# Reserving a PSUM bank only where it is used, and moving the feed-forward's statistics behind the softmax division

## The chip, the cores and the metric

The kernel runs on one core of a Trainium2 chip. The metric is the device time of one execution in microseconds, taken as the median of several runs; less is better. The engines named below are TensorE (PE in the profile), VectorE (DVE), ScalarE (ACT), GpSimd (POOL) and the queue of SyncE (SP), which issues the DMAs of the main path.

## The reference, cut to what matters

The input has two batches of 256 times, 128 bands and 128 channels, in float32. Three residual blocks follow one another: causal attention over time, attention over bands with a mask that lets each band see 16 neighbours on either side, and a feed-forward with 512 hidden channels.

```python
B, T, FB, C = (2, 256, 128, 128)
H_T, H_F, BAND = (4, 4, 16)
INNER = 4 * C
xt = _ln(x, ln_t_w, ln_t_b).transpose(0, 2, 1, 3)
x = x + _mha(xt, t_wi, t_bi, t_wo, t_bo, H_T, cm).transpose(0, 2, 1, 3)
xf = _ln(x, ln_f_w, ln_f_b)
x = x + _mha(xf, f_wi, f_bi, f_wo, f_bo, H_F, bm)
xn = _ln(x, ln_n_w, ln_n_b)
h = jax.nn.gelu(xn @ w1.T + b1, approximate=False)
x = x + (h @ w2.T + b2)
```

## The kernel before

**Groups.** The work is cut into groups of 4 tiles of 128 x 128. First come 128 groups of time attention (`OverTime`). Then come 16 runs, each of 8 groups of band attention (`OverBands`) followed by the 8 groups of the feed-forward (`FeedForward`) on the same data; the feed-forward group that stands 8 places behind a band group reads that group's result `x2`. The change touches only the 16 runs.

**Steps.** `run` (line 1058) is one loop over steps n. Each step calls parts of several groups, and every instruction is pinned to the order in which it is emitted on its engine (`InOrder`, line 872). In this document the steps of one run are numbered 0 to 15: band groups are at home in steps 0 to 7, feed-forward groups in steps 8 to 15. Step 8 is the turn (`turn` in the code, line 1083).

**What one band step does.** TensorE: scores of group n (into four banks `sp`), the softmax sums `rp` and weighted values `op` of group n-1 (`weigh`, line 803; the profile's `bank<-pf,ones` and `bank<-pf,v`), the output product `yp` of group n-2 (`bank<-wn,oT`), then queries `qp`, keys `kp` and values `vp` of group n+1. ScalarE: four exponentials, then logarithm and exponential of `rp` (`invert`, line 607), then copies of queries, keys and values. POOL: the two small instructions of `root` (line 456) for feed-forward group n+4, and then six selects that mask the exponentials of heads 0 to 2 (`first_mask`, line 789). `root` comes first in POOL's order. Head 3 is masked by VectorE instead.

**VectorE in a band step**, in order: `first_function` (line 779, `bank<-bank,band`, the mask of head 3), `normalize` (four `xh`) and `turn` (one transpose `z`) for group n+3, `statistics` (line 447: four `stats`, four `mv`) of feed-forward group n+5, `finish` (line 641, `x<-bank,x`) of group n-2, and `divide` (line 620) of group n-1. `divide` has three instructions: `bank<-bank,r` works inside the bank of `rp`; `u<-bank,r` is the last that reads this bank; `oT<-bank,u` reads the bank of `op` and makes the input of the next step's output product. In steps 0 to 2 group n+5 is still a band group, so there are no feed-forward statistics; in steps 3 to 8 there are. In step 8 an exact reciprocal of `rp` (3.32 us, `invert_exactly`) comes before `finish` and `divide`.

**What follows the statistics.** The `mv` of group g, made at step g-5, are read by POOL's `root` at step g-4; VectorE normalizes the group at step g-3.

**Banks.** PSUM has 8 banks. On these steps they are handed out in turn (`turn_of_bank`, line 915), and a bank is written again only when all earlier users are through. `weigh` of a band group takes two turns ahead, before `rp` and `op`: one for `yp`, which this step's `output` uses, and one for `qp`, which this step's `queries_keys` uses (lines 579, 637 and 806). In steps 7 and 8 no band group follows whose queries could use the second. The bank reserved in step 8 stays in `path.held` and is taken in step 15 by the queries of the next run's first group.

The turns of steps 7 and 8 are then, in order: step 7, four `sp`, `yp`, `qp` (unused), `rp`, `op`; step 8, four `hp` (hidden layer of feed-forward group 8), `yp`, `qp` (unused there), `rp`, `op`. A step with 8 turns gives each tile the bank that its counterpart had a step earlier.

Of the kernel before, what the change touches and what calls it, by code (L numbers as in the profile page):

```python
# [427 lines left out]
class Group:  # L428
# [121 lines left out]
    def weigh(self):  # L550
        pass
# [95 lines left out]
def rows_of(h):  # L647
    return slice(h * D, (h + 1) * D)
# [95 lines left out]
def time_scores(old, new):  # L744


    if new is not None:
        new.first_tiles()
    if old is not None:
        old.second_tiles()  # L750
    for kind, h, s, e in TIME_ORDER:
        if kind == "s" and old is not None:
            old.second_scores(int(h), int(s), int(e) * HALF)
        if kind == "f" and new is not None:
            new.first_scores(int(h), int(s), int(e) * HALF)


class OverBands(Attention):


    which = 1
    by_vector = 1

    def scores(self, heads):
# [38 lines left out]
    def weigh(self):  # L803
        path = self.path

        path.held = dict(yp=path.turn_of_bank(), qp=path.turn_of_bank())
        self.rp = path.bank([P, NT * P], "rp")
        for h in range(H):
            path.tensor.matmul(
                self.rp[rows_of(h), :], path.k.ones[:, 0:D], self.p[:, h].rearrange("p i q -> p (i q)"),  # L810
                start=True, stop=True,
            )
        self.op = path.bank([P, NT * P], "op")
        for i in range(NT):
            c = slice(i * P, (i + 1) * P)
            for h in range(H):
                r = rows_of(h)
                path.tensor.matmul(self.op[r, c], self.v[:, i, r], self.p[:, h, i, :], start=True, stop=True)
# [68 lines left out]
class BoundedPath:  # L887
# [170 lines left out]
    def run(self, x, out):  # L1058
        groups = list(self.groups(x, out))

        def do(n, *names):
            if 0 <= n < len(groups):
                for name in names:
                    getattr(groups[n], name)()

        def at(n, kind):
            return 0 <= n < len(groups) and isinstance(groups[n], kind)

        def do_at(n, kind, *names):
            if at(n, kind):  # L1070
                do(n, *names)


        run0 = [i for i in range(len(groups)) if at(i, OverBands)][: RUN // NT]
        due = dict(zip(run0, (-5, -4, -4, -3, -1, 0, 1, 2)))
        due = {n: [i for i in run0 if run0[0] + due[i] == n] for n in range(-12, len(groups) + 2)}
        A = RUN // NT

        self.scalar.preload_act_table_set(EXP_SET)
        for n in range(-12, len(groups) + 2):  # L1080
            feeds = [at(n - 2 + i, FeedForward) for i in range(5)]
            bands = [at(n - 2 + i, OverBands) for i in range(5)]
            turn = feeds[2] and bands[1]
            old, new = (groups[i] if at(i, OverTime) else None for i in (n, n + 1))
            if bands[2] and feeds[1]:
                self.scalar.preload_act_table_set(EXP_SET)
            do_at(n + 4, FeedForward, "root")
            do(n, "first_half", "first_function", "first_mask")
            if n >= 0:
                do_at(n + 5, OverTime, "statistics")  # L1090
            if old is not None or new is not None:
                time_scores(old, new)
                b = self.banks
                Attention.place = dict(rp=b["b0"], op=b["b3"], yp=b["a1"], qp=b["a2"], kp=b["b1"], vp=b["b2"])
            else:
                Attention.place = {}
            if old is not None:
                old.second_weights(old.late)
            if new is not None:
                new.first_weights(new.early[:1])  # L1100
            if old is not None:
                old.second_weights(old.early)
                old.mask_second()
                old.add(0)
                old.add(1)
            if new is not None:
                new.first_weights(new.early[1:])
            if n >= 0:
                do_at(n + 5, OverTime, "root_in_bank")
            if turn:  # L1110
                do(n, "second_half", "second_function")
            do_at(n + 3, OverTime, "fetch")
            do_at(n + 2, (OverBands, FeedForward), "fetch")

            for i in (2 * n + 12, 2 * n + 13) if n < -2 else (n + 10,) if n < 2 else ():
                if i >= NT:
                    do(i, "load")
            if n < -8 or n >= 0:
                do(n + 12, "load")
            if n >= 0:  # L1120
                for i in due[n]:
                    do(i, "statistics")
            do_at(n + 3, (OverBands, FeedForward), "normalize", "turn")
            do_at(n + 4, OverTime, "normalize", "turn")
            if n >= 0:
                do_at(n + 5, OverTime, "refine")
            if n < 0:
                do(n + 5, "statistics")
            do_at(n + 5, FeedForward, "statistics")
            if n == -4:  # L1130
                self.fold_rest()
                self.warm()
            do(n - 1, "weigh")
            do(n - 1, "invert_exactly" if turn else "invert")
            if new is not None:
                new.first_weights(new.late)
            if bands[2] or turn or old is not None:
                do(n - 2, "output", "finish")
            do(n - 1, "divide")
            if not turn:  # L1140
                do(n, "second_half", "second_function")
            if n in run0:
                do(n, "bias")
            if not bands[2] and old is None:
                do_at(n, FeedForward, "bias")
                do_at(n + A, OverBands, "bias")
                if at(n - 1, FeedForward) and at(n - 2, OverBands):
                    do_at(n + A - 1, OverBands, "statistics", "root")
                if not turn:
                    do_at(n + A, OverBands, "statistics", "root")  # L1150
            do_at(n + 2, OverTime, "queries_keys", "take_query", "take_key")
            do_at(n + 1, OverBands, "queries_keys", "take_query", "take_key")
            if n < 0:
                do_at(n + 5, OverTime, "root_by_scalar", "refine")
            for i in due[n]:
                do(i, "root_by_scalar", "refine")
            do_at(n, OverTime, "bias")
            if new is not None:
                new.mask_first()
            if not bands[2] and not turn and old is None:  # L1160
                do(n - 2, "output", "finish")
            do_at(n + 2, OverTime, "values", "take_values")
            do_at(n + 1, OverBands, "values", "take_values")
            if old is not None or new is not None:

                b = self.banks
                self.banks = dict(
                    a1=b["a1"], a2=b["a2"], b0=b["a0"], b3=b["a3"], a0=b["b0"], a3=b["b1"], b1=b["b3"], b2=b["b2"]
                )
# [69 lines left out]
```

## Time and profile before

| | before |
|---|---|
| median of 3 runs | 2682.34 us (2681.44 to 2683.59) |
| the profiled execution | 2680.03 us, of which the span of its trace is 2678.2 us |
| granted TensorE clock | 0.999 |
| VectorE busy | 2190.0 us (82%) |
| POOL busy | 1951.5 us (73%) |
| ScalarE busy | 1856.2 us (69%) |
| one run of 16 steps, start to start (1282.67 to 1390.10 us) | 107.43 us |

Busy times are shares of the whole span, in which three kinds of work follow one another, so they don't say which engine limits a stage. The starts of one recurring instruction say it better: the interval between two `bank<-pf,ones` is what a band step costs TensorE, and the interval between two `bank<-bank,band` is what it costs VectorE.

### The profile page before, as it was taken

What the parts mean: (1) busy time and instruction counts of PE and PEld (TensorE: products, weight loads), DVE (VectorE), ACT (ScalarE), POOL (GpSimd) and SP (SyncE); (2) the same over time, 40 slices, a digit from 0 to 9 for tenths busy, and PEclk for the clock granted to TensorE, in tenths of its full rate; (3) what the DMA queues carried; (4) which work ended last, traced back from release to release, by engine and by line L of the source; (5) the groups of instructions that cost most, each with busy time, mean ns of one, the idle gap of its engine ahead of it and who ended that gap; (6) DMA issues with size and microseconds to landing.
All of it is one profiled execution on the core that took longest, in us unless ns stands there. A gap on an engine that the chain in (4) does not pass through costs nothing.

```text
span 2678.2 us, 156630 instructions
## 1 busy us (share of the span) xinstructions
PE 2639.5 (99%) x68662; PEld 1801.7 (67%) x68662; DVE 2190.0 (82%) x6708; ACT 1856.2 (69%) x3620; POOL 1951.5 (73%) x2297
## 2 busy tenths in 40 slices
PE   7999999999999999999999999999999999999998
PEld 5666666666666666666666666666666667666665
DVE  6888898988889996967868769688687696886874
ACT  6999999999999874664755746647557466475573
POOL 4999999999999886766667657666676576666762
PEclk9999999999999999999999999999999999999999
DMA  6556555555555544445445444454454544544533
GB/s 151 151 150 157 145 154 155 149 150 152 150 151 150 132 115 125 121 115 132 111 120 132 112 123 121 119 132 110 121 133 109 123 124 114 136 109 122 131 96 83
DMA packets 471511, 347.09 MB, mean 130 GB/s; under 512 B 43296, under 2 KB 405152, under 8 KB 470816
## 3 DMA queue, kind: packets, MB, share of 16 engines
q1 hardware_dynamic: 469568, 335.92, 48.9%
q8 instruction: 540, 8.85, 1.5%
q14 instruction: 155, 1.27, 0.2%
q10 hardware_dynamic: 1248, 1.05, 0.2%
HBM read 169.03 MB, written 167.77 MB: 126 GB/s over the span
## 4 chain that ended last, share of the span: by engine, by line
PE 80%; DVE 15%; DMA 2%; issue 1%; SPq 1%; ACT 0%; DVEq 0%; ACTq 0%
PE bank L882 80%; DVE xh L882 3%; DVE bank L882 3%; DVE stats L882 2%; DVE z L882 2%; DVE u L882 2%; DMA xnT<-turned 1%; DVE x L882 1%; DMA turned<-z 1%; DVE mv L882 1%; SPq L882 1%; DVE oT L882 0%; ACT p L882 0%; DVE vy L882 0%; DVE res L882 0%
## 5 line engine op out<-in xcount | busy, mean ns | idle before, releaser
L882 ACT ACTIVATE hT<-bank,b 128x512 f32<-128x512 f32 x512 | 347.0, 688 | 536.1 <-PE bank L882 518.0
L882 POOL TENSOR_SCALAR_AFFINE_SELECT pf<-pf 128x512 f32<-128x512 f32 x768 | 478.0, 637 | 244.8 <-ACT pf L882 218.4
L882 DVE TENSOR_SCALAR xh<-x,mv,rstd 128x160 f32<-128x160 f32 x1536 | 596.6, 430 | 14.2
L882 PEld LDWEIGHTS bank<-w2T_sb,hT 128*32 128x32 f32 x16384 | 459.3, 110 | 62.9 <-issue 38.8
L882 PE MATMUL bank<-xnT,wf 128*32 128x512 f32 x4096 | 487.6, 592 | 3.0 <-ACT p L882 3.0
L882 PE MATMUL bank<-w2T_sb,hT 128*32 128x128 f32 x16384 | 477.2, 273 | 0.4 <-ACT hT L882 0.2
L882 PE MATMUL bank<-xnT,w1f 128*32 128x512 f32 x4096 | 474.5, 592 | 0.0
L882 ACT ACTIVATE p<-bank 128x512 f32<-128x512 f32 (+1 forms) x1024 | 430.6, 494 | 37.9 <-PE bank L882 26.7
L882 POOL TENSOR_SCALAR_AFFINE_SELECT p<-p 128x1024 f32<-128x1024 f32 (+2 forms) x384 | 364.5, 950 | 83.5 <-ACT p L882 75.0
L882 DVE TENSOR_TENSOR res<-bank,res 128x512 f32<-128x512 f32 x256 | 175.8, 687 | 289.7 <-PE bank L882 230.2
L882 PEld LDWEIGHTS bank<-wf,xnT 128*32 128x32 f32 x8192 | 234.0, 110 | 155.8 <-issue 103.0
L882 POOL TENSOR_TENSOR p<-p,p 128x512 f32<-128x512 f32 x256 | 324.3, 1289 | 10.7
L882 PE MATMUL bank<-qT,kT 32*64 32x80 f32 (+4 forms) x16384 | 323.7, 273 | 4.0 <-DVE oT L882 2.4
L882 DVE BATCH_NORM_STATS2 stats<-x 128x6 f32<-128x128 f32 x1536 | 326.3, 274 | 0.1
L882 PEld LDWEIGHTS bank<-qT,kT 32*64 32x64 f32 x16384 | 275.9, 131 | 58.2 <-ACT kT L882 48.4
L882 ACT ACTIVATE pf<-bank 128x512 f32<-128x512 f32 x512 | 267.0, 602 | 50.7 <-PE bank L882 49.0
L882 DVE STREAM_TRANSPOSE z<-xh 128x512 f32<-128x512 f32 x384 | 273.2, 711 | 13.5
L882 PEld LDWEIGHTS bank<-xnT,w1f 128*32 128x32 f32 x4096 | 156.8, 110 | 189.3 <-issue 158.3
L882 POOL TENSOR_SCALAR rstd<-mv 128x4 f32<-128x4 f32 x248 | 56.7, 229 | 311.0 <-DVE mv L882 309.8
L882 PE MATMUL bank<-wn,oT 128*32 128x128 f32 x8192 | 272.0, 273 | 0.0
L882 POOL TENSOR_TENSOR rstd<-rstd,mhalf 128x4 f32<-128x4 f32 x248 | 256.9, 1036 | 20.7
L882 PE MATMUL bank<-wf,xnT 128*32 128x128 f32 x8192 | 271.6, 273 | 0.0
(97 smaller groups left out, 3653.3 us busy)
## 6 DMA issues: line engine op xcount, KB each, us to landing
turned<-z SPq DMA_DIRECT2D x1536, 64.0 KB, 2.5
xnT<-turned SPq DMA_DIRECT2D x384, 256.0 KB, 3.2
x<-in_x SPq DMA_DIRECT2D x128, 256.0 KB, 4.3
x<-res SPq DMA_DIRECT2D x256, 128.0 KB, 2.4
x<-x SPq DMA_DIRECT2D x128, 256.0 KB, 4.3
out<-res SPq DMA_DIRECT2D x256, 128.0 KB, 2.5
w1T_sb<-in_w1T ACTq DMA_DIRECT2D x1, 256.0 KB, 5.7
w2T_sb<-in_w2T ACTq DMA_DIRECT2D x1, 256.0 KB, 7.3
```

What stands on the lines that cost most here:

```text
L882: return self.tc.keep_in_program_order(emit(*args, **kwargs))
```

## The change

There are two edits. In `weigh`, a band group takes a turn for `yp` always, and one for `qp` only where the group two places on is also a band group: in steps 1 to 6 of a run, not in steps 7 and 8. The queries of a run's first group take the bank in turn, since none is held for them.

In steps 3 to 8, `statistics` of the feed-forward is emitted behind `divide` of group n-1, where before it stood ahead of `weigh`. On VectorE the order of a band step becomes `first_function`, `xh`, `z`, `x`, the three instructions of `divide`, `stats`, `mv`. In the feed-forward steps from 9 on it stays where it was. No instruction is added or left out.

```diff
@@ class OverBands
     which = 1
+    follow = ("yp",)
     by_vector = 1
@@ def weigh(self):
-        path.held = dict(yp=path.turn_of_bank(), qp=path.turn_of_bank())
+        path.held = {name: path.turn_of_bank() for name in self.follow}
         self.rp = path.bank([P, NT * P], "rp")
@@ def run(self, x, out):
+        for i in range(len(groups) - 2):
+            if at(i, OverBands) and at(i + 2, OverBands):
+                groups[i].follow = ("yp", "qp")
@@ in the loop over n
-            do_at(n + 5, FeedForward, "statistics")
+            if not bands[2] and not turn:
+                do_at(n + 5, FeedForward, "statistics")
...
             if bands[2] or turn or old is not None:
                 do(n - 2, "output", "finish")
             do(n - 1, "divide")
+            if bands[2] or turn:
+                do_at(n + 5, FeedForward, "statistics")
```

## Prediction

> **What bounds the kernel now.** I read the page first: its busy times, then TensorE's groups.
>
> ```profile
> PE 2639.5 (99%) x68662; PEld 1801.7 (67%) x68662; DVE 2190.0 (82%) x6708; ACT 1856.2 (69%) x3620; POOL 1951.5 (73%) x2297
> ...
> L882 PE MATMUL bank<-pf,ones 128*32 128x512 f32 x1024 | 136.7, 604 | 12.4 <-DVE u L882 12.4
> ```
>
> TensorE is idle for 38.7 us of the 2678.2. By the page's slices 13 to 20 us of that lie in the first fortieth of the span and some in the last, so a change to the runs has little to gain. One idle time recurs: 12.4 us ahead of the softmax sums `rp`, released by VectorE's `u`. The view of waits gives its count.
>
> ```profile
> PE bank L882 <- DVE u L882: 12.8, 17, 0.8
> ```
>
> One of the 17 (0.35 us at 934 us) lies in the time attention; the other 16 are one per run. The timeline of one run, TensorE first (start, duration, instructions), shows where, and the reader should look at the starts:
>
> ```profile
> 1426.14 1.20 PE L882 MATMUL bank<-qT,kT 32*64 32x80 f32 x64
> 1427.27 1.06 PE L882 MATMUL bank<-pf,ones 128*32 128x512 f32 x8
> 1428.15 1.06 PE L882 MATMUL bank<-pf,v 128*32 128x128 f32 x32
> 1429.03 1.06 PE L882 MATMUL bank<-wn,oT 128*32 128x128 f32 x32
> 1429.90 3.62 PE L882 MATMUL bank<-xnT,w1f 128*32 128x512 f32 x32
> 1434.31 1.06 PE L882 MATMUL bank<-pf,ones 128*32 128x512 f32 x8 [0.79 <-DVE u L882]
> ```
>
> The idle 0.79 us is at step 8, the turn. The same view of VectorE, from step 7's first instruction on:
>
> ```profile
> 1428.28 0.69 DVE L882 SCALAR_TENSOR_TENSOR bank<-bank,band 128x512 f32<-128x512 f32 x1
> 1428.88 1.60 DVE L882 TENSOR_SCALAR xh<-x,mv,rstd 128x160 f32<-128x160 f32 x4
> 1430.51 0.71 DVE L882 STREAM_TRANSPOSE z<-xh 128x512 f32<-128x512 f32 x1
> 1431.15 0.83 DVE L882 BATCH_NORM_STATS2 stats<-x 128x6 f32<-128x128 f32 x4
> 1431.90 0.36 DVE L882 BATCH_NORM_AGGREGATE mv<-stats 128x2 f32<-128x6 f32 x4
> 1432.18 0.66 DVE L882 TENSOR_TENSOR x<-bank,x 128x512 f32<-128x512 f32 x1
> 1432.75 0.69 DVE L882 TENSOR_TENSOR bank<-bank,r 128x512 f32<-128x512 f32 x1
> 1433.47 0.69 DVE L882 SCALAR_TENSOR_TENSOR u<-bank,r 128x512 f32<-128x512 f32 x1
> 1434.20 0.69 DVE L882 TENSOR_TENSOR oT<-bank,u 128x512 f32<-128x512 f32 x1
> ```
>
> VectorE has no gap. From `bank<-bank,band` to the next it takes 6.53 us in steps 3 to 7 of every run, while TensorE's steps take 6.3 (6.32 from step 4's `bank<-pf,ones` to step 5's and from there to step 6's, as means over the runs): VectorE is the slower engine there, falls 0.2 us further behind per step, and is caught at step 8. The last view is POOL in steps 6 and 7:
>
> ```profile
> 1425.82 0.23 POOL L882 TENSOR_SCALAR rstd<-mv 128x4 f32<-128x4 f32 x1 [0.26 <-DVE mv L882]
> 1426.13 1.04 POOL L882 TENSOR_TENSOR rstd<-rstd,mhalf 128x4 f32<-128x4 f32 x1
> 1428.10 3.94 POOL L882 TENSOR_SCALAR_AFFINE_SELECT pf<-pf 128x512 f32<-128x512 f32 x6 [0.92 <-ACT pf L882]
> 1432.35 0.23 POOL L882 TENSOR_SCALAR rstd<-mv 128x4 f32<-128x4 f32 x1 [0.31 <-DVE mv L882]
> 1432.66 1.03 POOL L882 TENSOR_TENSOR rstd<-rstd,mhalf 128x4 f32<-128x4 f32 x1
> 1433.66 1.28 POOL L882 TENSOR_TENSOR res<-x,rows_sb 128x512 f32<-128x512 f32 x1
> ```
>
> The root is done before the exponentials arrive, so the selects wait for ScalarE, and end at 1432.04, over 2 us before TensorE reads them at 1434.31.
>
> **What the Trainium skill says.** "PSUM — Partial Sum Buffer", section "Engine vs sequencer instructions": the queues of ScalarE, VectorE and GpSimd are strict first-in first-out, and matmuls start in program order. The trace agrees: POOL's selects never pass the root ahead of them, and a late `rp` holds all of step 8's products. "Perfetto Trace Analysis", section "Optimization Strategy", takes a gap that repeats on the saturated engine as a hint at too few buffers; the 16 gaps of 0.61 to 0.84 us on a bank fit. "SBUF — State Buffer", section "SBUF: two separate sides": VectorE and GpSimd share a port pair as an exclusive lock, which a VectorE instruction with two SBUF inputs takes. In this trace, at 919.73 us, a 128x4 `vy` beside a POOL select took 1.01 us against 0.16 elsewhere. Feed-forward statistics have one SBUF input and took 0.83 us for four beside selects (1424.62) and 0.86 beside an idle POOL (1464.75); this is why I let durations stand when the order changes.
>
> **The change part by part.** *The bank.* Before, steps 7 and 8 take 8 turns each, so step 8's `rp` falls on step 7's `rp`, whose last reader is `u`: 1433.47 + 0.69 + 0.15 of release = 1434.31. After, they take 7 each. Eight turns back from step 8's `rp` is now step 7's `yp`, free with `x` at 1432.84; `op` gets step 7's `rp`, but is written 0.85 later; `yp` gets the fourth `sp`. TensorE could start `rp` at 1429.90 + 2 x 1.72 (what 16 products of that kind take, 1436.91 to 1438.63) = 1433.34. With this edit alone `op`'s wait sets 1434.31 - 0.85 = 1433.46, a gain of 0.85. Of this step 9 takes some back: its output product, at 1443.84 before, would come to 1442.99, and `oT` of step 8 ends at 1442.60 + 0.43, with release 1443.18. So 0.66 us per run, 10.6 in all. The bank in step 15: the queries get one last used in step 14, and the four `sp` of step 0 get banks whose readers ran in step 15, ahead of the keys which the scores need anyway; I cost it at nothing.
>
> *The statistics.* VectorE's sum stays; 1.03 us (1432.18 - 1431.15) move from ahead of `x` to behind `oT`. So `x`, `u` and `oT` end 1.03 earlier, and `bank<-bank,band` stays where it was. `u` is then free for step 8 at 1433.28, and the second `oT` at 1442.0, so neither of the two waits above is left, whichever bank is used. It also frees 0.17: step 7's scores at 1426.14 take 1.20 instead of some 1.0, since their third bank is step 6's `yp`, read by `x` until 1426.31. Does a moved instruction now wait? `x` would start at 1431.15 and its product ended at 1430.09; `bank<-bank,r` at 1431.72 and ScalarE's `r` ended at 1430.75. In step 3, where VectorE is least behind, 1405.04 against 1404.72 and 1405.62 against 1405.24. No. Neither moved nor passed instructions issue a DMA here (a band group has no store), so SP's queue is untouched.
>
> What it delays is POOL: `root` stands ahead of the selects, and now waits for `mv` made at the end of VectorE's step. Call the start of step p's `bank<-bank,band` zero. The `mv` end at 0.08 (as `mv` now end 0.08 after `x` starts), plus 0.09 release (1432.26 to 1432.35), plus 1.31 from `rstd` to POOL's next start, plus 3.94 for six selects, plus 0.15 release to TensorE, taken from `u`: 5.57. Heads 0 and 1 of the sums can issue before, which I put at 0.02. So TensorE's next `rp` comes at 5.55 at the earliest. In step 7's frame before it came at 1434.31 - 1428.28 = 6.03 (6.02 to 6.04 in all 16 runs). Unhindered it would be 5.1. The root's chain is the wait that takes the old one's place, and the gain is 6.03 - 5.55 = 0.48 us per run. One step earlier it gives 1421.76 + 5.55 = 1427.31 against 1427.27 before, so the freed 0.17 is lost; two steps earlier 1420.78 against 1420.81. The delays aren't added up, since all hang on VectorE's clock, which doesn't wait for TensorE in these steps. The late `mv` of step 8 hold up step 9's root and the `res` behind it by about 5 us; this `res` is read in step 10 and has that slack (it starts at 1439.60 before, near 1444.5 then, and is read at 1452.78).
>
> Sum: 16 x 0.48 = 7.7 us. The profiled execution of 2680.03 (span 2678.2 and 1.8 around it) would become 2672.3; the median shown is 2.3 above it, so 2682.34 - 7.7 = 2674.6 us. In this the first edit is worth next to nothing beside the second.
>
> **The rivals.** *TensorE alone is left.* If POOL's chain is shorter than I sum it, or the sums needn't wait for it, `rp` starts near 1433.3, 1.0 earlier, and 16 us go: 2666.3. For it speaks that releases from POOL aren't shown; against, that I would have to be wrong by 0.4 of 5.55. *Nothing moves.* If the chain is 0.35 longer (slower release, or the wait of all four heads together), 0.13 x 16 = 2 us are left: 2680.3. *Slower.* The root now runs at VectorE's `xh` (430 ns each) instead of its division. Should the port lock make POOL's power and one select each wait for an `xh`, the chain is 0.86 longer: 6.41, that is 0.38 later than now, 16 x 0.38 = 6.1 us: 2688.4. It decides from 0.48 on. Against it: `xh` beside selects (1428.88) and beside roots (1449.49) take 1.60 for four, and the selects 637 ns, so no hold shows.
>
> **How the numbers follow.** Forecast 0.58, TensorE alone 0.14, nothing moves 0.17, slower 0.11. About 0.2%, 5.4 us, is what a measurement of this kernel tells from no change. The forecast passes it while the chain stays under 5.69, and I leave 0.03 of its 0.58 beyond that: faster 0.69, same 0.20, slower 0.11. The range takes in half of either neighbour, 2668.5 to 2680.5; the forecast's own, with 0.12 us of doubt in the chain, is 2672.7 to 2676.6.
>
> **What would show it.** Right: step 8's `rp` starts 5.45 to 5.65 after step 7's `bank<-bank,band`; POOL's root stands idle for `mv`, and its selects follow without a gap; no wait on `u` is left; VectorE's steps stay at 6.53. Wrong: VectorE's steps lengthen, selects wait for ScalarE as before, or TensorE gets a new idle time in steps 9 to 15.

## The result, and the profile after

The changed kernel takes 2672.96 us (median of 7 runs, 2671.05 to 2675.60) against 2682.48 us of the kernel before, measured beside it. The ratio is 0.9964, with a 95% interval of 0.9953 to 0.9976: 9.5 us less, where 7.7 was forecast. The profiled execution's span went from 2678.2 to 2669.3 us.

Busy times on the page of the changed kernel say nothing of a gain, with one exception to keep in mind: weight loads (PEld) are busy 132 us longer, with as many instructions.

```profile
PE 2638.6 (99%) x68662; PEld 1934.0 (72%) x68662; DVE 2190.2 (82%) x6708; ACT 1855.8 (70%) x3620; POOL 1948.0 (73%) x2297
```

The view of TensorE's waits in the changed kernel (total, times, longest):

```profile
PE bank L883 <- DVE oT L883: 6.6, 16, 2.1
...
PE bank L883 <- DVE u L883: 0.3, 1, 0.3
```

The 16 waits on `u` at the turn are gone. In their place stand 14 waits on `oT` ahead of `rp`, 4.1 us in all by the view of groups (two more on `oT`, 2.4 us together, and the one left on `u` lie in the time attention, as before). TensorE's timeline of one run shows steps 7 and 8:

```profile
1532.49 1.06 PE L883 MATMUL bank<-pf,ones 128*32 128x512 f32 x8 [0.28 <-DVE oT L883]
...
1535.09 3.64 PE L883 MATMUL bank<-xnT,w1f 128*32 128x512 f32 x32
1538.52 1.32 PE L883 MATMUL bank<-pf,ones 128*32 128x512 f32 x8
1539.38 1.12 PE L883 MATMUL bank<-pf,v 128*32 128x128 f32 x28
1540.25 0.31 PE L883 MATMUL bank<-wn,oT 128*32 128x128 f32 x2
1540.33 0.28 PE L883 MATMUL bank<-pf,v 128*32 128x128 f32 x2
```

The new wait is in step 7, at 1532.49. Step 8's `rp`, at 1538.52, follows its predecessor without idle time, but takes 1.32 us instead of 1.06, and the last lines are out of the program's order: an output product starts before the last weighted values. TensorE's output is cut into four column tiles here, one per head in `rp`; each head's sums leave two records. Taken one by one, the first records of heads 0 and 1 start at 1538.52 and 1538.56, those of heads 2 and 3 at 1538.79 and 1538.80 (the program's order tells which head is which). So two columns are late, and the other two have gone ahead. VectorE and POOL in the same run show who makes them late:

```profile
1531.65 0.69 DVE L883 TENSOR_TENSOR oT<-bank,u 128x512 f32<-128x512 f32 x1
1532.26 0.86 DVE L883 BATCH_NORM_STATS2 stats<-x 128x6 f32<-128x128 f32 x4
1533.03 0.36 DVE L883 BATCH_NORM_AGGREGATE mv<-stats 128x2 f32<-128x6 f32 x4
1533.31 0.67 DVE L883 SCALAR_TENSOR_TENSOR bank<-bank,band 128x512 f32<-128x512 f32 x1
```

```profile
1533.48 0.23 POOL L883 TENSOR_SCALAR rstd<-mv 128x4 f32<-128x4 f32 x1 [1.30 <-DVE mv L883]
1533.79 1.04 POOL L883 TENSOR_TENSOR rstd<-rstd,mhalf 128x4 f32<-128x4 f32 x1
1534.81 3.93 POOL L883 TENSOR_SCALAR_AFFINE_SELECT pf<-pf 128x512 f32<-128x512 f32 x6
```

POOL's root stands idle 1.30 us for `mv`, its selects follow without a gap, and end at 1538.74, which is 0.22 after `rp` began. That is head 2's mask, the last one. Head 2's sums start 0.05 us later, 5.48 after `bank<-bank,band` (median of runs 2 to 16). Head 3's mask is made by VectorE at 1533.31, ahead of its exponential, so no select holds it; yet its sums start only with head 2's, which stand ahead of them in the program. The step 7 wait is `oT`'s end, 1531.65 + 0.69 = 1532.34, plus 0.15.

### The profile page after: what moved, and what is told of

It reads as the page before. It is cut to its first block, busy times and chain, and to the rows that moved or that the text cites. A ratio compares the mean times of both kernels' runs of the same rounds, so it can differ in the third digit from the quotient of the medians.

```text
span 2669.3 us, 156675 instructions
## 1 busy us (share of the span) xinstructions
PE 2638.6 (99%) x68662; PEld 1934.0 (72%) x68662; DVE 2190.2 (82%) x6708; ACT 1855.8 (70%) x3620; POOL 1948.0 (73%) x2297
## 3 DMA queue, kind: packets, MB, share of 16 engines
q14 instruction: 155, 1.27, 0.2%
## 4 chain that ended last, share of the span: by engine, by line
PE 84%; DVE 12%; DMA 2%; issue 1%; ACT 0%; SPq 0%; POOL 0%; DVEq 0%; ACTq 0%
PE bank L883 84%; DVE xh L883 2%; DVE bank L883 2%; DVE u L883 1%; DVE oT L883 1%; DVE z L883 1%; DVE stats L883 1%; DMA xnT<-turned 1%; DVE x L883 1%; DVE mv L883 0%; DMA turned<-z 0%; SPq L883 0%; DMA x<-in_x 0%; ACT p L883 0%; DVE vy L883 0%
## 5 line engine op out<-in xcount | busy, mean ns | idle before, releaser
L883 PEld LDWEIGHTS bank<-w2T_sb,hT 128*32 128x32 f32 x16384 | 496.7, 110 | 25.3 <-issue 15.4
L883 PE MATMUL bank<-xnT,w1f 128*32 128x512 f32 x4096 | 508.0, 592 | 0.0
L883 PE MATMUL bank<-w2T_sb,hT 128*32 128x128 f32 x16384 | 503.2, 273 | 0.3 <-issue 0.2
L883 PE MATMUL bank<-xnT,wf 128*32 128x512 f32 x4096 | 494.1, 592 | 3.1 <-ACT p L883 3.1
L883 PEld LDWEIGHTS bank<-wf,xnT 128*32 128x32 f32 x8192 | 245.2, 110 | 142.6 <-issue 100.7
L883 PEld LDWEIGHTS bank<-xnT,w1f 128*32 128x32 f32 x4096 | 244.5, 110 | 129.6 <-issue 93.1
L883 PE MATMUL bank<-wn,oT 128*32 128x128 f32 x8192 | 281.0, 273 | 0.0
L883 PE MATMUL bank<-wf,xnT 128*32 128x128 f32 x8192 | 278.1, 273 | 0.0
```

Of the source, the lines that this page charges most:

```text
L883: return self.tc.keep_in_program_order(emit(*args, **kwargs))
```

## The experiments

Four intervals tell the kernels apart. They were read from the timelines of the runs: step 7's `rp` from step 6's `bank<-bank,band`, step 8's `rp` from step 7's `bank<-bank,band` (medians), step 3's `rp` to step 8's, and step 8's `rp` to the first `rp` of the next run (means). The first of the 16 runs is left out; its third interval is 1.0 to 1.8 us longer than the mean of the others. Times in us; an `rp` starts with heads 0 and 1; each median stands for its own kernel, and ratios are to the kernel before on the same chip.

| kernel | median | step 7 `rp` | step 8 `rp` | 3 to 8 | 8 to next run |
|---|---|---|---|---|---|
| before | 2682.5 | 5.52 | 6.03 | 32.43 | 63.14 |
| changed | 2673.0 | 5.71 | 5.21 | 31.70 | 63.22 |
| banks alone | 2684.1 | 6.76 | 6.27 | 32.68 | 62.96 |
| statistics alone | 2674.5 | 5.37 | 4.99 | 31.53 | 63.56 |
| statistics, bank given up in step 8 only | 2673.2 | 5.37 | 4.89 | 31.40 | 63.49 |
| changed, root behind selects | 2667.4 | 5.72 | 5.21 | 31.69 | 62.94 |
| step 8 only, root behind selects | 2660.9 | 5.37 | 4.89 | 31.39 | 62.97 |
| before, fresh bank in step 15 | 2680.2 | 5.52 | 6.03 | 32.44 | 62.98 |
| changed, root behind, four selects more | 2687.0 | 5.71 | 5.21 | 31.69 | 64.12 |
| statistics, root behind selects | 2668.7 | 5.37 | 4.99 | 31.56 | 63.10 |

**The bank edit alone.** The statistics stay in front:

```diff
-            if not bands[2] and not turn:
-                do_at(n + 5, FeedForward, "statistics")
+            do_at(n + 5, FeedForward, "statistics")
...
-            if bands[2] or turn:
-                do_at(n + 5, FeedForward, "statistics")
```

> Only the bank edit; the statistics stay ahead of the division. The prediction's working: the wait on u at step 8 goes and about 0.66 us per run are gained, 10.6 us, so about 2672. Theory formed from the trace of the changed kernel: the edit also moves step 7's rp onto the bank of step 6's op, which oT reads last; with the division not moved forward, oT ends 6.6 us after step 6's bank<-bank,band, so step 7's rp starts about 6.75 after it (5.52 in the kernel before), and step 8's rp about 6.27 after step 7's bank<-bank,band (6.03 before): about 0.24 us per run lost, 3.8 us, so about 2686.

Measured: 2684.09 us, ratio 1.0006 (0.9997 to 1.0014). No gain, against 10.6 us by the prediction. The theory of the banks gave 6.75 and 6.27 for the two intervals and 6.76 and 6.27 were found. In TensorE's timeline of this kernel step 7 now waits over a microsecond:

```profile
1539.32 1.07 PE L883 MATMUL bank<-pf,ones 128*32 128x512 f32 x8 [1.14 <-DVE oT L883]
```

The expected loss of 3.8 us came out as 1.8, within the interval of no difference; the last column says why. It fell by 0.18 us where nothing was expected. This is the start of the sixth experiment.

**The statistics alone.** All banks as before:

```diff
-            if at(i, OverBands) and at(i + 2, OverBands):
+            if at(i, OverBands):
                 groups[i].follow = ("yp", "qp")
```

> Only the statistics moved; both banks are reserved in every band step as before. The prediction's theory (POOL's root and selects bind at 5.55, the bank edit is worth nothing): the same time as the changed kernel, 2673. Theory of the banks: step 7's rp no longer waits for oT and starts at about 5.4 after step 6's bank<-bank,band (5.73 in the changed kernel), step 8's rp waits for u and starts 4.99 after step 7's (5.20): 0.21 us per run faster than the changed kernel, 3.4 us, so about 2669.5.

**The bank given up in step 8 only.**

```diff
-            if at(i, OverBands) and at(i + 2, OverBands):
+            if at(i, OverBands) and at(i + 1, OverBands):
                 groups[i].follow = ("yp", "qp")
```

> Statistics moved, and the bank for queries given up in step 8 only, still reserved in step 7. The prediction's theory: POOL binds, 2673 as the changed kernel. Theory of the banks: neither oT nor u is waited for; step 7's rp near 5.4, step 8's near 4.9 after the bank<-bank,band of the step before: 0.3 us per run faster than the changed kernel, 4.8 us, so about 2668.

Measured: 2674.53 us for the statistics alone (ratio 0.9969, 0.9957 to 0.9982) and 2673.22 us for the bank given up in step 8 only (0.9960, 0.9946 to 0.9973). The starts of `rp` came where the banks put them, 4.99 and 4.89. But the times didn't follow: within the noise both kernels are as fast as the changed one (2672.96), as the prediction's theory had it. What `rp` gained was lost again in the last column of the table, 63.56 and 63.49; of the first, some 0.18 is a wait in step 15, which the sixth experiment explains. In TensorE's timeline of the kernel that gives the bank up in step 8 only, the late columns show:

```profile
1540.02 1.24 PE L883 MATMUL bank<-pf,ones 128*32 128x512 f32 x6
1540.88 0.39 PE L883 MATMUL bank<-pf,v 128*32 128x128 f32 x4
1541.09 0.60 PE L883 MATMUL bank<-pf,ones 128*32 128x512 f32 x2
```

Two of the eight `rp` records start at 1541.09, behind four weighted values. They are the second records of heads 2 and 3, whose first started at 1540.64, when the selects were through (1540.58). So an earlier `rp` only makes heads 2 and 3 lag more, and the theory of the banks was right on the starts and wrong on the time.

**The root behind the selects.** Both edits, and POOL's order changed in band steps:

```diff
-            do_at(n + 4, FeedForward, "root")
+            if not bands[2]:
+                do_at(n + 4, FeedForward, "root")
             do(n, "first_half", "first_function", "first_mask")
+            if bands[2]:
+                do_at(n + 4, FeedForward, "root")
```

> The changed kernel with POOL's root emitted behind the selects in band steps, so that the selects start when ScalarE is through, over 1 us earlier. The prediction's theory: the wait that it named is gone, step 8's rp starts near 5.1 after step 7's bank<-bank,band and some 6 us more are gained, about 2666.5. Theory of the banks: step 7's rp still waits for oT at 5.72, step 8's stays at 5.20, and the time is that of the changed kernel within 1.5 us, about 2672; only the late third column of step 8's sums goes.

Measured: 2667.41 us, ratio 0.9941 (0.9927 to 0.9955), 5.6 us less than the changed kernel (4.6 by the intervals). Each theory had one half right. `rp` still starts at 5.72 and 5.21, as the banks say; the time fell as POOL's chain says. On POOL's timeline of this kernel the selects wait for ScalarE again, and the root follows them:

```profile
1533.63 3.93 POOL L883 TENSOR_SCALAR_AFFINE_SELECT pf<-pf 128x512 f32<-128x512 f32 x6 [1.11 <-ACT pf L883]
1537.53 0.23 POOL L883 TENSOR_SCALAR rstd<-mv 128x4 f32<-128x4 f32 x1
```

TensorE's `rp` of the same step takes 1.07 us, with no split lines behind it:

```profile
1539.22 1.07 PE L883 MATMUL bank<-pf,ones 128*32 128x512 f32 x8
```

The theory after these four: there are two waits side by side, VectorE's through the banks on the start of `rp`, and POOL's through head 2 on the columns of heads 2 and 3, and the later of them is paid.

**Neither wait left.** The bank given up in step 8 only, and the root behind the selects: the two diffs above together.

> Statistics behind the division, the bank for queries given up in step 8 only, and POOL's root behind the selects. Theory formed from the first four runs: two waits end side by side, VectorE's through the banks (start of rp) and POOL's through head 2 (its column of the array), and the later one is paid. Here neither is left: step 8's rp near 4.9 after step 7's bank<-bank,band, and from there to the next run's first rp 62.95 us; 0.3 us per run less than with both edits and the root behind the selects, 4.9 us, so about 2662.5. Rival, that TensorE is at its own pace already in that kernel: 2667.

Measured: 2660.87 us, ratio 0.9919 (0.9905 to 0.9932). It is the fastest of all, 21.7 us below the kernel before. In TensorE's timeline of a run the two steps have neither an idle time nor a late column:

```profile
1529.44 1.06 PE L883 MATMUL bank<-pf,ones 128*32 128x512 f32 x8
...
1535.51 1.04 PE L883 MATMUL bank<-pf,ones 128*32 128x512 f32 x8
```

By the intervals it stands 0.27 us per run below the kernel with both edits and the root behind the selects (31.39 + 62.97 against 31.69 + 62.94), 4.3 us of the 6.5 between the medians. The profiled executions, also 6.5 us apart, show where the rest lies. From the first `rp` of the bands to the last they take 1642.2 and 1637.0 us, 5.2 apart; the first run alone, left out of the intervals, gives 1.1 of it. The time attention, which no edit touches, ended 1.3 us earlier: the first `rp` of the bands started at 960.7 and 959.4 in these two, and between 957.2 and 961.3 in all ten profiled executions.

**A fresh bank in step 15.** The kernel before, with one line in `FeedForward.weigh`:

```diff
         path, NI = self.path, self.path.k.NI
+        path.held.pop("qp", None)
         self.zp = path.bank([P, NT, P], "zp")
```

> The kernel before, with nothing changed but that the bank held since step 8 is forgotten in step 9, so that the queries of step 15 take a bank in turn; all turns of steps 7 and 8 stay. Theory: in step 15 the values' bank is the queries' own, and the values wait some 0.18 us for ScalarE's qT; this goes, 16 x 0.18 = 2.9 us, so about 2679.4, and the time from step 8's rp to the next run's first falls from 63.14 to about 62.95. The prediction's working, which costed this at nothing: 2682.3.

Measured: 2680.15 us, ratio 0.9990 (0.9983 to 0.9996), so 2.4 us less where 2.9 were expected. In the kernel before, TensorE starts the values (the second line) 1.89 us after the queries:

```profile
1593.46 1.93 PE L882 MATMUL bank<-xnT,wf 128*32 128x512 f32 x16
1595.35 1.08 PE L882 MATMUL bank<-wf,xnT 128*32 128x128 f32 x32
```

ScalarE takes the queries out of their bank at the same time, and ends at 1595.30:

```profile
1594.61 0.69 ACT L882 ACTIVATE qT<-bank,bq 128x512 f32<-128x512 f32 x1 [0.20 <-PE bank L882]
```

With the fresh bank the same two lines of TensorE are 1.72 us apart:

```profile
1595.06 1.93 PE L883 MATMUL bank<-xnT,wf 128*32 128x512 f32 x16
1596.78 1.08 PE L883 MATMUL bank<-wf,xnT 128*32 128x128 f32 x32
```

Counting turns explains it. The held bank was handed out in step 8, and the values' turn in step 15 comes exactly 40 turns later, five rounds of eight: the same bank.

**Head 2 made later still.** Both edits with the root behind the selects, and head 2's last select repeated four times in step 7:

```diff
+        for i in range(4 if self.last else 0):
+            path.gpsimd.affine_select(
+                out=blk, in_=blk, compare_op=ALU.is_ge, fill=path.zero, base=BAND,
+                pattern=[[0, NT], [1, P]], channel_multiplier=-1,
+            )
```

> Both edits and the root behind the selects, and in step 7 of each run head 2's second select is done four times more on the same data, which changes no value. Its end moves from about 1.7 us ahead of step 8's rp to about 1.0 us behind its start. Theory (a late head is paid in full, though the other columns of the array go on): step 8's rp stays at 5.21 after step 7's bank<-bank,band, the time from there to the next run's first rp grows from 62.94 to about 63.9, and 16 us are lost: about 2683. Rival (what one column lags is made up beside the others' work): 2667 as without them.

Measured: 2687.00 us, ratio 1.0017 (1.0010 to 1.0023), 19.6 us more than without the repeats. `rp` still starts at 5.21. From there to the next run it takes 64.12 us, 1.18 more than without them, 18.9 us over 16 runs. TensorE and POOL in one run:

```profile
1543.87 1.05 PE L889 MATMUL bank<-pf,ones 128*32 128x512 f32 x4
1545.08 0.62 PE L889 MATMUL bank<-pf,ones 128*32 128x512 f32 x2 [0.15 <-POOL pf L889]
1545.10 0.63 PE L889 MATMUL bank<-pf,v 128*32 128x128 f32 x8
1545.54 0.60 PE L889 MATMUL bank<-pf,ones 128*32 128x512 f32 x2
```

```profile
1538.28 6.75 POOL L889 TENSOR_SCALAR_AFFINE_SELECT pf<-pf 128x512 f32<-128x512 f32 x10 [1.11 <-ACT pf L889]
```

The selects end at 1545.03. Head 2's and head 3's sums start at 1545.08 and 1545.09, and only behind them, at 1545.10, the weighted values of heads 0 and 1, whose own masks were done earlier. Of the 1.2 us that head 2 is behind heads 0 and 1 only 0.15 show as idle time, yet all of it is paid by the next run. The delay is paid in full.

**Statistics and root moved, banks as before.**

> Statistics behind the division and POOL's root behind the selects, all banks as in the kernel before. Theory: step 8's rp waits for u and starts 4.99 after step 7's bank<-bank,band, and the values of step 15 wait 0.18 us for their bank: about 0.27 us per run slower than with the bank given up in step 8 only, 4.3 us, so about 2667. Rival, the prediction's view that the bank edit is worth nothing beside the statistics: the same time as with the bank given up in step 8 only.

Measured: 2668.71 us, ratio 0.9949 (0.9935 to 0.9963), against 2660.87 with the bank given up in step 8 only. So the bank is worth something once POOL's chain is out of the way: 0.17 us per run up to step 8, and 0.13 behind it, where step 15 has its wait again: 4.8 us by the intervals, where 4.3 were expected. The medians show 7.8; in the profiled executions the bands take 5.6 us longer, and the time attention ended 1.2 us later.

## Why the prediction was right, and where it was not

**POOL's chain: right, and it set the gain.** The prediction had head 2's sums start 5.57 us after `bank<-bank,band`, and `rp` as a whole 0.02 ahead of that. In the changed kernel head 2's sums start at 5.48. The difference lies in the last term: the release from POOL to TensorE, taken as 0.15 from VectorE's, is 0.05 (1538.74 to 1538.79). `rp` itself starts at 5.21, and the late columns add 63.22 - 62.96 = 0.26 behind it (62.96 is the mean of the four kernels without late columns and with a fresh bank in step 15), which makes 5.47. The net gain of this term is 32.43 - 31.70 - 0.26 = 0.47 us per run, against 0.48.

In its form the step was wrong: it let heads 0 and 1 start no more than 0.02 ahead, and they started 0.27 ahead. It drew on the rule of the Trainium skill ("PSUM — Partial Sum Buffer", section "Engine vs sequencer instructions") that matmuls start in program order. This trace agrees only as far as the wait itself, where head 3's sums stay behind head 2's. Later the columns of heads 0 and 1 run ahead of matmuls that stand earlier in the program, output products at 1540.25 ahead of weighted values at 1540.33, and the idle time that a reader would look for isn't there. So the named sign for a right forecast, `rp` between 5.45 and 5.65, did not occur, though head 2's start lies there.

**Step 7: the wait on `oT` was missed.** "TensorE alone" and the forecast both counted the turns of step 8 only. Step 7 has one turn less ahead of its `rp` too, and eight turns back from it lies step 6's `op`, whose reader `oT` is VectorE's last in the division. It costs the changed kernel nothing by itself, since POOL's chain ends later still (the kernel with the bank kept in step 7 is as fast), but it is why 0.66 us per run for the bank edit alone was wrong: step 7 lost 1.24 us there, against 1.00 won at the turn (the mean from step 7's `rp` to step 8's was 7.03 us before, and is 6.03).

**Step 15: a bank costed at nothing was worth 0.18 us per run** (63.14 - 62.96). The prediction looked at who had used the queries' bank before, and not at who used it next. The fresh bank alone saved 2.4 us. It is also all that the bank edit adds to the statistics in the changed kernel: the last two columns together are 95.09 us for the statistics alone and 94.92 for both edits.

**VectorE's sum stays: nearly.** Its four steps from step 3's `bank<-bank,band` to step 7's went from 26.13 to 26.23 us; four `stats` take 0.86 instead of 0.83. That is 0.10 us per run, 1.6 in all. No instruction that moved forward has a new wait in the run shown, as forecast, and in steps 9 to 15 of all runs TensorE is idle once, for 0.2 us, as before.

**The sum.** Per run 0.73 were won up to step 8, 0.26 given back by the late columns, and 0.18 came from step 15: 0.65, as the intervals show it (107.33 to 106.68 from run to run), 10.4 us in 16 runs. From the first `rp` of the bands to the last the profiled executions show 10.8 (1657.1 to 1646.3). Their spans show 8.9, since the time attention, which the change doesn't touch, ended 1.9 us later. The forecast of 7.7 lacked step 15, 2.9 us. Its other errors nearly cancel: POOL's chain was 0.08 us shorter than forecast, and VectorE's steps 0.10 longer. The cause of the gain was forecast; that the two errors cancel is luck, and so is part of the closeness to the measured 9.5, since the end of the time attention scatters by more than the 1.8 us between them.

**The rivals.** TensorE alone, 2666.3, was what the root behind the selects brought within reach: the prediction named the right obstacle. The slower one, a port lock that lengthens POOL's chain, is refuted: six selects take 3.93 us in the changed kernel and took 3.94 in the kernel before, and the root's second instruction beside `xh` takes 1.04 us against 1.03.

## What to carry to other kernels

When a rotation of buffers gets a turn less, count eight turns back for every tile that follows, not for the one whose wait you mean to remove, and for a bank held across steps also look for the next user. When an instruction is moved back on one engine, follow its result to the queue where it is waited for, and see what stands behind it there; here a small root at the head of POOL's queue cost some 5 us until it stood behind the selects. Judge a wait by the time from one recurring instruction to the same one a round later, since the start of the waiting group can improve while the round does not.

## What the runs showed of the hardware

With the products cut into four column tiles of 32, a late operand held what stands behind it in the program until its own product started: with four selects more, head 3's sums waited for head 2's (1545.09 behind 1545.08), and the weighted values of heads 0 and 1 for both (1545.10). From there on the columns kept their own pace, and the early ones overtook: in the changed kernel output products start at 1540.25, ahead of weighted values at 1540.33.

How far the early columns got ahead can be read at step 9's last products, `bank<-w2T_sb,hT`. The times are from step 8's `rp` to the first and the last of them, means of runs 2 to 15.

| kernel | first | last |
|---|---|---|
| changed, root behind selects (no late columns) | 4.32 | 7.76 |
| changed | 4.32 | 7.99 |
| statistics, bank given up in step 8 only | 4.55 | 8.31 |
| changed, root behind, four selects more | 5.15 | 8.94 |

Against the first row the late columns are 0.23, 0.32 and 0.35 us further behind the early ones. What head 2 was late beyond that, all columns lost at once: 0.83 of the 1.18 us with four selects more. Why the lead ended there wasn't tried.

In the changed kernel the late columns keep their lag through all feed-forward steps of a run, some 50 us, without idle time in TensorE's row (in step 15 the last of these products still comes 0.23 us later, 50.43 against 50.20). It is paid at the scores with which the next run begins, which read what ScalarE copied from all four columns: they start 1.27 us after the values of step 15 (1592.20 to 1593.47), and 1.01 us with the root behind the selects (1592.91 to 1593.92).

The busy time of weight loads is a sign of columns out of step, and no measure of the lag. A single load of 128x32 takes 110 ns in the changed kernel as before; the busy time counts overlapping loads once, so it grows when they overlap less. It is 1934.0 us in the changed kernel, 1828.3 to 1836.9 in the other three with late columns, the least with the longest delay, and 1777.8 to 1812.1 in the six without.
